# Conditioned residual layer on one core: tiles reordered on chip so that 25 pairs share a matrix, and the pair-matrix products done as seven half products

## The chip, the cores and the metric

The kernel runs on one core of a Trainium2 chip, in float32. The metric is the device time of one execution in microseconds (us), the median of several runs. The engines are called as in the profile: PE is TensorE's matmul, PEld its weight load, DVE is VectorE, ACT is ScalarE, POOL is GpSimd, and SP is the queue that issues most plain DMAs. L404 is line 404 of the kernel before.

## The reference, cut to what matters

The input `x` has 16 x 512 tokens of 512 features. Every token has a pathway id (500), a compartment id `c` (5, used also as time step) and a scale type `m` (3 in the tables; the mask that is passed in holds only 0 and 1).

```python
h = ln(x, pw_g[pathway], pw_b[pathway]);  h = ln(h, cp_g[c], cp_b[c])
t = ln(x, tm_g[c], tm_b[c]);              s = ln(x, ms_g[m], ms_b[m])
mm, n, r = [x + mlp_ln(state)[:, None, :] for state in (memory, noise, resource)]
cat = concat([w0*h, w1*t, w2*mm, w3*n, w4*r, w5*s], -1)       # w = softmax(aw)
out = x + ln(silu(cat @ int_W1 + int_b1) @ int_W2 + int_b2, int_g, int_be)
```

`t` and `s` are the same normalised `x` with another scale for each column. So for all tokens of one group (c, m) the two blocks of `int_W1` fold into one 512 x 512 matrix V = diag(w1 tm_g[c]) W1_t + diag(w5 ms_g[m]) W1_s. The three `x +` blocks fold into one matrix for `x`, and what hangs on batch and group becomes one added row for each token.

## The kernel before, in words

The kernel sorts the 8192 tokens on chip by group (15 groups, NG) and cuts the sorted list into 64 tiles of 128 tokens. The group of a tile is that of the token in its middle; tokens of another group at a border are put right by correction rows. A window is four tiles, and 16 windows are worked off one after another. In window w, tiles g = 0 and 2 are tiles 2w and 2w+1 of the sorted list, and g = 1 and 3 are tiles 32+2w and 33+2w (`by_place`, `PLACES`).

For a window, rows of `x` (`gx`), of the pathway table (`gh`), of the compartment table (`gc`) and the added rows (`ga`) are gathered by indirect DMAs from POOL. ACT and DVE make the sums and norms (`xs`, `f1`, `fs`, `f2`, `fn`, `nv`; the powers `xp`, `fp`, `lp` are POOL's). Each tile is turned in two steps: a 32 x 32 block transpose on DVE (`tx`, `tv`, `th`, `tz`, L197) and four DMAs of SP for each tile (`sX`, `sV`, `sH`, `sZ`, L205), which fill `catX`, `catV`, `catH`, `catZ`. All four block transposes of a window must be done before the first of its SP rows.

First layer, for each tile, three products of 128 x 512 by 512 x 512: with V (`lV`, `layer1`, L404, four matmuls of 512 columns, each of two records in the trace), and with the matrices of `x` and `h`. The last two are done from window 1 on as a Strassen-Winograd scheme: two tiles of a window form a pair p (tiles 2p and 2p+1), the two rows of a 2 x 2 block matrix whose columns are X and H. Seven products of half width (`m7.w.p.k`, `half_product`, L452, four matmuls of 256 columns each) stand for eight. DVE makes the token sums in place (`u1` to `u4`) and adds the parts that several results share (`r1`, `r2`, `r3`, `r5`, `half_out`). The V products and the parts that belong to one result gather in a PSUM bank for each tile (`p1`), the shared parts in a bank for each pair (`u`). Then come the sum with the gathered row (`ha`, L472), silu (`hs`, L475), turning (`tz`, `sZ`) and the second layer, seven products again (`q7.w.p.k`, L546, two matmuls of 256 columns each) with sums on POOL (`zs`, L532 to L538) and a bias put in first (`kb`, L520). The result is taken out of PSUM (`kf`, `sf`, `ku`, `sl`), normalised (`lq`, `lv`, `lp`, `lb`) and scattered to the output (`po`).

The V of a tile lies in `vs[g % 2]`. It is built only when the group changes from the tile of the same parity before: ACT writes W1_s scaled (`sp`, `s_part`, L257) and DVE adds W1_t scaled (`bd`, `build`, L265), both under a branch on a flag that is loaded into registers (`va`, `vd`).

The order of work on every engine is written out: `ORDER` for the start, `WINDOW` for each later window and `LAST` for the last one. A name such as `lV.c.1` is a piece for the current window (c; p is the window before, o the one before that, n the next, m the one after) and tile 1. Every engine takes its instructions strictly in that order. Before `ORDER`, a straight-line part counts the groups, gives every token its place (`pos`, L832), and makes the sorted list by comparing places with `i_q` (the tile numbers 0 to 63) and multiplying one-hot matrices on PE (`one_hots`, L883 to L896). From it come the gather indices `tok`.

Of the kernel before, what the change touches and what calls it, by code (L numbers as in the profile page):

```python
# [1548 lines left out]
```

## Time and profile before

| | |
|---|---|
| time, median of 3 runs | 923.6 us (922.99 to 923.74) |
| profiled execution, first to last instruction | 920.3 us |
| its own time: that span and about 3.3 us around it, taken from the median | about 923.6 us |
| PE busy | 884.8 us (96%) |
| PEld busy | 642.0 us (70%) |
| DVE busy | 733.6 us (80%) |
| ACT busy | 521.2 us (57%) |
| POOL busy | 666.9 us (72%) |
| DMA | 185.40 MB, mean 201 GB/s |
| builds of a V (L265 x44, four for each) | 11 |

A share of busy time is a mean over stages with different limits; the table by stage, asked for with stretches of about one window, says which engine has no room in which stage. The chain that ended last runs backwards from the last instruction to what released each step. Busy times there are counted once where records of one engine overlap, and the mean of one instruction is its whole record.

### The profile page before, as it was taken

The numbers are of one execution on the slowest core, as the hardware profiler recorded it, in microseconds if no ns is written. First come the engines' busy times: TensorE is split into PE (matmuls) and PEld (weight loads), VectorE is DVE, ScalarE is ACT, GpSimd is POOL, SyncE is SP. The second block draws the span as 40 slices with busy tenths as digits, with TensorE's granted clock in tenths as the row PEclk, the third lists the DMA queues.
The fourth block names the chain that finished last, engine by engine and source line by source line (L and its number), as shares of the span: only waits on it lengthen the run. The fifth ranks groups of instructions, "written<-read, shape, count | busy, mean of one in ns | idle before, by whom it ended". The sixth has DMA issues, their size and how long they took to land.

```text
span 920.3 us, 13563 instructions
## 1 busy us (share of the span) xinstructions
PE 884.8 (96%) x3617; PEld 642.0 (70%) x3617; DVE 733.6 (80%) x1360; ACT 521.2 (57%) x1263; POOL 666.9 (72%) x730
## 2 busy tenths in 40 slices
PE   6979899999999999999999999999999999999996
PEld 6634446868677777868686877777686867778682
DVE  8776767878789798978787887869697888879565
ACT  5568736464555738374646556473657566572413
POOL 9876678576768678686878686877767676876452
PEclk9999999999999999999999999999999999999999
DMA  8755677777767777777777777777667776776513
GB/s 272 249 185 179 220 226 197 207 210 204 235 178 232 202 218 195 215 208 202 227 202 227 187 235 191 226 193 216 186 197 210 203 220 191 221 200 190 154 37 113
DMA packets 88557, 185.40 MB, mean 201 GB/s; under 512 B 24324, under 2 KB 24388, under 8 KB 88476
## 3 DMA queue, kind: packets, MB, share of 16 engines
q0 software_dynamic: 31104, 104.88, 39.4%
q1 hardware_dynamic: 56668, 79.53, 29.6%
q8 instruction: 30, 0.49, 0.2%
q14 instruction: 51, 0.42, 0.2%
q10 hardware_dynamic: 704, 0.08, 0.1%
HBM read 100.48 MB, written 19.97 MB: 131 GB/s over the span
## 4 chain that ended last, share of the span: by engine, by line
PE 50%; POOL 5%; DVE 4%; issue 3%; DMA 3%; SPq 2%; ACT 1%; POOLq 0%; DVEq 0%; ACTq 0%
PE u L452 13%; PE p L404 13%; PE p L452 11%; PE pq_0b L546 4%; PE pq_1b L546 4%; PE pq_1a L546 3%; PE pq_0a L546 2%; SPq L205 2%; DMA catZ<-rZ 2%; POOL xbs L391 1%; POOL out L638 1%; DMA pw<-in_pw,i_pw 1%; DVE vs L265 1%; DVE yb L634 0%; DVE yb L633 0%
## 5 line engine op out<-in xcount | busy, mean ns | idle before, releaser
L404 PE MATMUL p<-vs,catV 128*128 128x512 f32 x512 | 228.3, 593 | 3.9 <-DVE vs L265 1.7
L404 PEld LDWEIGHTS p<-vs,catV 128*128 128x128 f32 x512 | 96.9, 190 | 108.5 <-issue 99.6
L452 PE MATMUL p<-wh__81,catH 128*128 128x256 f32 x480 | 111.0, 379 | 0.0
L452 PEld LDWEIGHTS p<-wh__81,catH 128*128 128x128 f32 x480 | 91.4, 190 | 12.2
L376 ACT ACTIVATE pw<-pw,rsh 128x512 f32<-128x512 f32 x64 | 45.6, 714 | 95.2 <-DVE pw L383 76.9
L638 POOL DMA_INDIRECT out<-yb,tok x64 | 75.4, 1178 | 31.2 <-issue 15.1
L475 ACT ACTIVATE add<-add 128x512 f32<-128x512 f32 x64 | 39.7, 625 | 94.4 <-DVE add L472 93.1
L350 ACT ACTIVATE junk<-pw 128x512 bf16<-128x512 f32 x60 | 37.5, 626 | 85.8 <-DVE pw L347 78.1
L171 POOL DMA_INDIRECT cp<-cp_rows,i_cp x64 | 73.4, 1147 | 15.5 <-issue 13.2
L391 POOL TENSOR_TENSOR xbs<-xbs,rows 128x512 f32<-128x512 f32 x64 | 82.4, 1289 | 1.4
L171 POOL DMA_INDIRECT pw<-in_pw,i_pw x64 | 63.0, 984 | 28.1 <-DVE rH L197 13.0
L625 POOL TENSOR_TENSOR rsy<-vey,mhalf 128x4 f32<-128x4 f32 (+1 forms) x16 | 23.6, 1473 | 82.3 <-DVE veh L368 69.5
L171 POOL DMA_INDIRECT xbs<-in_x,tok x64 | 65.1, 1017 | 19.9 <-issue 18.1
L171 POOL DMA_INDIRECT add<-rows,i_add x64 | 67.0, 1048 | 16.6 <-issue 16.5
L383 DVE SCALAR_TENSOR_TENSOR pw<-pw,sumsh,cp 128x512 f32<-128x512 f32 x60 | 45.5, 760 | 32.9 <-DMA cp<-cp_rows,i_cp 32.8
L317 ACT ACTIVATE xm<-xbs,nmx,rsx 128x512 f32<-128x512 f32 x64 | 48.8, 806 | 22.9 <-DVE nmx L311 17.2
L372 POOL TENSOR_TENSOR rsh<-veh,mhalf 128x1 f32<-128x1 f32 x64 | 48.6, 760 | 13.0 <-DVE veh L368 11.5
L347 DVE SCALAR_TENSOR_TENSOR pw<-pw,rsx 128x512 f32<-128x512 f32 x64 | 56.0, 876 | 2.3
L452 PE MATMUL p<-wt,catH 128*128 128x256 f32 x240 | 56.7, 379 | 0.0
L452 PE MATMUL u<-wt,catX 128*128 128x256 f32 x240 | 56.5, 379 | 0.0
L452 PEld LDWEIGHTS u<-wx__80,catX 128*128 128x128 f32 x240 | 45.7, 190 | 12.6 <-issue 3.8
L452 PE MATMUL u<-wt,ss 128*128 128x256 f32 x240 | 54.4, 379 | 0.0
(439 smaller groups left out, 2127.7 us busy)
## 6 DMA issues: line engine op xcount, KB each, us to landing
catX<-rX SPq DMA_DIRECT2D x240, 64.0 KB
catV<-rV SPq DMA_DIRECT2D x240, 64.0 KB
catZ<-rZ SPq DMA_DIRECT2D x240, 64.0 KB
catH<-rH SPq DMA_DIRECT2D x240, 64.0 KB
rows<-adde SPq DMA_DIRECT2D x8, 256.0 KB
yb<-in_int_W SPq DMA_DIRECT2D x1, 1024.0 KB
catH<-in_int_W SPq DMA_DIRECT2D x1, 1024.0 KB
w1x<-in_int_W SPq DMA_DIRECT2D x1, 1024.0 KB
```

The costliest lines, as they stand in the source:

```text
L171: nc.gpsimd.indirect_dma_start(dst, None, table, bass.IndirectOffsetOnAxis(ap=idx, axis=0), **kw)
L317: nc.scalar.activation(t, st["xb"][:, j, :], AF.Identity, bias=st["nm"][:, j : j + 1], scale=st["rs"][:, j : j + 1])
L347: nc.vector.scalar_tensor_tensor(h, h, st["rs"][:, j : j + 1], pw[:, D:], ALU.mult, ALU.add)
L372: nc.gpsimd.tensor_tensor(rs, st.pop(("ve", j)), mhalf[:, :1], ALU.pow)
L376: nc.scalar.mul(pw[:, :D], pw[:, :D], st.pop(("rs", j)))
L383: nc.vector.scalar_tensor_tensor(pw[:, :D], pw[:, :D], st["sh", j][:, 1], cp, ALU.add, ALU.mult)
L391: nc.gpsimd.tensor_add(st["xb"][:, j, :], st["xb"][:, j, :], rows[:, 2, :])
L404: nc.tensor.matmul(st["p1", g], st["c" + blk][:, g, c, :], m[:, c, :], start=(blk == first and c == order[0]), stop=(blk == last and c == ...
L452: nc.tensor.matmul(dst, m[:, c], at_["half1"][k][:, c], start=(k == 1 and c == 0), stop=(c == NC - 1), skip_group_check=True)
L475: nc.scalar.activation(st["add", g], st["add", g], AF.Silu)
L546: nc.tensor.matmul(st["pq", 2 * p + i][:, half], st["zp", p][k][:, c], at_["half"][k][:, c], start=False, stop=(c == 1), skip_group_check= ...
L638: nc.gpsimd.indirect_dma_start(out_rows[j], bass.IndirectOffsetOnAxis(ap=tok[:, j, w : w + 1], axis=0), yb[:, j, :], None)
```

## The change

The 64 tiles are put into another order. A group's tiles are taken two by two, all pairs come first, and tiles that are left over alone come last. This is worked out on chip: from the group borders follows how many tiles each group has, whether that is odd (`n_odd`), and with that the tile for each place (`i_q` is overwritten with it, and `by_place` now takes four places in a row for a window). At most 14 groups can have a tile alone, so 25 pairs (`PURE`) surely share one V. With the inputs of the reference the groups have 11, 11, 11, 11, 12, 1, 2, 2, 2 and 1 tiles; there are 29 such pairs, the other four are treated as single tiles.

For a pair that shares its V, the V product of both tiles is a product of a 2 x 2 block matrix (two tiles by two halves of the features) with V in four quarters, done by seven products of two matmuls with 256 columns (`v7.w.p.k`, `norm_product`). Its parts fall into the same places as those of `m7`, so both add up in the same PSUM halves. New sums of the turned tiles are made by DVE (`yv`, four of 128 x 256 for each pair, in the buffer of `rV`), and new sums of V's quarters by DVE when V is built (four more instructions; they take the place of `vs[1]`). The first shared part is no longer added by DVE (`r1` goes); ACT copies it from PSUM into both halves of the tile's bank before the other parts add up there (`cf`, `copy_first`). Places 50 to 63 use `lW` (`whole_product`), as `lV` before. Window 0 keeps whole products. So 23 pairs (windows 1 to 11, and the first of window 12) use `v7`.

`ORDER`, `WINDOW` and `LAST` are new; `LAST` writes out windows 12 to 15 by number, `ORDER` now reaches to the middle of window 1's work. The store of the sorted list to `in_order` becomes an indirect DMA on POOL behind the first gathers of `x`, because its rows are in the new order.

```diff
 WINDOW = """
+    m7.p.0.2 u4.p.0 fp.c.1 fn.c.1 u1.p.1 m7.p.1.2 m7.p.0.6 u4.p.1 m7.p.1.6 lp.o lb.o.3 kb.p.0 r2.p.0 kz.m.2 po.o.3 va.n
+    lb.o.0 gx.n.0 m7.p.1.5 sp.c.0 bd.c.0 m7.p.0.5 sh.p.0 r5.p.1 gc.c.3 lb.o.2 sV.c.3 gx.n.2 xs.n.0 gx.n.3 r3.p.1
+    m7.p.0.3 m7.p.1.4 th.c.1 ha.p.0 r2.p.1 u3.c.0 ha.p.3 hs.p.3 r3.p.0 gh.c.2 th.c.0 m7.p.0.4 ha.p.1 r5.p.0 hs.p.0
+    gh.c.3 hs.p.1 lb.o.1 tz.p.3 po.o.1 m7.c.0.1 v7.c.0.1 m7.p.1.3 tz.p.0 ha.p.2 po.o.2 cf.c.0 m7.c.0.7 v7.c.0.2 hs.p.2
+    sV.c.1 yv.c.0.3 gc.c.2 v7.c.0.7 kb.p.1 xs.n.3 tz.p.1 sh.p.1 sX.c.2 gx.n.1 tz.p.2 m7.c.1.1 ga.c.3 yv.c.0.1 cf.c.1
+    f1.c.2 v7.c.0.5 yv.c.0.2 yv.c.0.4 fs.c.2 f1.c.3 v7.c.0.3 fv.c.2 v7.c.0.6 sX.c.3 u3.c.1 ga.c.1 v7.c.0.4 sp.c.2 bd.c.2
+    v7.c.1.1 sZ.p.0 q7.p.0.1 q7.p.0.2 kz.p.1 fs.c.3 po.o.0 fv.c.3 fp.c.2 cf.c.2 m7.c.1.7 yv.c.1.3 f2.c.2 f2.c.3 sZ.p.1
+    xs.n.1 sh.c.3 fn.c.2 th.c.2 sZ.p.2 fp.c.3 fn.c.3 th.c.3 zs.p.0 tx.n.1 v7.c.1.7 q7.p.0.7 zs.p.1 q7.p.0.5 zs.p.2
...
+    PURE = (NT // P - (NG - 1)) // 2
...
+    def v_half(k):
+        if k in (4, 5, 6, 7):
+            return vs[1][:, {5: 0, 7: 1, 6: 2, 4: 3}[k]].rearrange("p (c n) -> p c n", c=2)
+        return vs[0][:, 2 * (k > 1) :, (k > 2) * (D // 2) :][:, :2, : D // 2]
...
+    def one_matrix(st, g):
+        return tile_of(st, g) - g % 2 < 2 * PURE
...
     def build(st, g):
-        w, v = st["w"], v_of(st, g)
+        if one_matrix(st, g) and g % 2:
+            return
+        w, v = st["w"], vs[g % 2]
...
                 nc.vector.scalar_tensor_tensor(v[:, c], wt[:, c], sct[:, c, g, w : w + 1], v[:, c], ALU.mult, ALU.add)
+            if one_matrix(st, g):
+                nc.vector.tensor_sub(v_half(5), b12, b11)
+                nc.vector.tensor_sub(v_half(7), b22, b12)
+                nc.vector.tensor_sub(v_half(6), b22, v_half(5))
+                nc.vector.tensor_sub(v_half(4), b21, v_half(6))
...
+    def norm_sum(st, p, k):
...
+            st["sv"] = catp.tile([P, 2, 4, 2, P], F32, tag="rotV", name=f"sv{st['w']}")
+        s1, s2, s3, s4 = [st["sv"][:, p, n] for n in range(4)]
+        a11, a12, a21, a22 = [st["cV"][:, 2 * p + r, 2 * n : 2 * n + 2] for r in range(2) for n in range(2)]
         if k == 1:
             nc.vector.tensor_add(s1, a21, a22)
         elif k == 2:
             nc.vector.tensor_sub(s2, s1, a11)
         elif k == 3:
+            nc.vector.tensor_sub(s3, a11, a21)
         else:
+            nc.vector.tensor_sub(s4, a12, s2)
...
+    def norm_product(st, p, k):
...
+        for c in range(2):
+            nc.tensor.matmul(dst, m[:, c], v_half(k)[:, c], start=(k == 5 and c == 0), stop=(c == 1),
+                             skip_group_check=True)
...
+    def copy_first(st, g):
...
+        nc.scalar.copy(st["p1", g].rearrange("p (k n) -> p k n", k=2),
+                       st["u", g // 2][:, :H].unsqueeze(1).to_broadcast([P, 2, H]))
...
-        if kind == "1":
-            nc.vector.tensor_add(a[:, :H], a[:, :H], u)
...
     def by_place(t):
-        return t.rearrange("p (b w a) -> p a b w", b=2, a=2)
+        return t.rearrange("p (w g) -> p g w", g=Q)
...
+    nc.vector.tensor_scalar(t_ends[:, 1:NG], row_beg, t_mid, None, ALU.is_gt)
+    nc.vector.tensor_sub(t_in, t_ends[:, 1:], t_ends[:, :NG])
     nc.vector.tensor_tensor(tmp, run, pc.unsqueeze(2).to_broadcast([P, NG, NQ]), ALU.add)
...
+    nc.tensor.matmul(pto[:NG, :1], t_in[:NQ], by_turns[:NQ], start=True, stop=True)
+    nc.scalar.activation(n_odd, pto[:NG, :1], AF.Square)
...
+    nc.vector.tensor_scalar(single, i_back[:NG], n_left, n_less, ALU.is_equal, ALU.mult)
...
+    nc.scalar.copy(i_q, pto[:, NQ : 2 * NQ])
...
+    for t, base in ((i_pos, 0), (i_mid, P // 2 - 1), (i_end, P - 1), (i_next, P)):
+        nc.gpsimd.tensor_scalar(t[:NB].rearrange("p (g w) -> p g w", g=Q), by_place(i_q[:NB]), float(P), float(base),
+                                ALU.mult, ALU.add)
...
-    nc.sync.dma_start(in_order.rearrange("(k r) o -> k (r o)", r=P), at_c)
...
     gather_x(w0)
+    nc.gpsimd.indirect_dma_start(in_order.rearrange("(k r) o -> k (r o)", r=P),
+                                 bass.IndirectOffsetOnAxis(ap=i_tile, axis=0), at_c, None)
...
-    for w in range(NW - 1):
+    for w in range(2, 12):
         run(WINDOW, w)
-    run(LAST, NW - 1)
+    run(LAST)
```

More of the change, by code (lines that the diff above doesn't have):

```diff
@@ L241, in changes, with tile_of @@
             skip_runtime_bounds_check_because="a comparison's result")
+    def tile_of(st, g):
+        return Q * st["w"] + g
+    def one_matrix(st, g):
+        return tile_of(st, g) - g % 2 < 2 * PURE
     def if_new(st, g, engine, part):
-        if st["w"] == 0 and g < 2:
+        if tile_of(st, g) in (0, 2 * PURE + 1):
             part()
@@ L260, in build @@
     def build(st, g):
-        w, v = st["w"], v_of(st, g)
+        if one_matrix(st, g) and g % 2:
+            return
+        w, v = st["w"], vs[g % 2]
+        H = D // 2
+        b11, b12, b21, b22 = [v[:, 2 * r : 2 * r + 2, k * H : (k + 1) * H] for r in range(2) for k in range(2)]
         def part():
@@ L404, in layer1 @@
             nc.tensor.matmul(st["p1", g], st["c" + blk][:, g, c, :], m[:, c, :],
-                             start=(blk == first and c == order[0]), stop=(blk == last and c == order[-1]),
-                             skip_group_check=st["w"] > 0)
+                             start=(blk == first and c == order[0]), stop=(blk == last and c == order[-1]))
     def awake(kind, at, n):
@@ L436, in token_sum, with home_of @@
         elif k == 3:
-            nc.vector.tensor_sub(a21, a11, a21)
+            nc.vector.tensor_sub(s3, a11, a21)
         else:
-            nc.vector.tensor_sub(a12, a12, s2)
+            nc.vector.tensor_sub(s4, a12, s2)
+    def home_of(st, p, k):
+        H = D // 2
+        key, half = {1: ("u", 0), 7: ("u", 0), 5: ("u", 0), 6: ("u", 1), 2: ("a", 0), 3: ("a", 1), 4: ("b", 0)}[k]
+        if key == "u":
+            if ("u", p) not in st:
+                st["u", p] = psum(f"u{st['w']}_{p}")
+            t = st["u", p]
+        else:
+            t = st["p1", 2 * p + (key == "b")]
+        return t[:, half * H : (half + 1) * H]
@@ new lines, in whole_product @@
+    def whole_product(st, g):
+        if one_matrix(st, g):
+            return
+        for c in range(NC):
+            nc.tensor.matmul(st["p1", g], st["cV"][:, g, c, :], vs[g % 2][:, c, :], start=False, stop=(c == NC - 1),
+                             skip_group_check=True)
+    def copy_first(st, g):
+        if ("p1", g) not in st:
+            st["p1", g] = psum(f"p1_{st['w']}_{g}")
+        H = D // 2
+        nc.scalar.copy(st["p1", g].rearrange("p (k n) -> p k n", k=2),
+                       st["u", g // 2][:, :H].unsqueeze(1).to_broadcast([P, 2, H]))
@@ L748 @@
     iota(i_rest[NH:], [[0, NQ]], base=NB1 - NH, step=1)
-    up = prep.tile([P, NG + 1], F32, name="up")
-    nc.gpsimd.memset(up[:, :1], 0.0)
     tokf = prep.tile([P, NE], F32, name="tokf")
@@ L783 @@
     nc.vector.memset(ones, 1.0)
+    odd_i = prep.tile([P, 1], I32, name="odd_i")
+    nc.vector.tensor_copy(odd_i, i_row)
+    nc.vector.tensor_scalar(odd_i, odd_i, 1, None, ALU.bitwise_and)
+    by_turns = prep.tile([P, 1], F32, name="by_turns")
+    nc.vector.tensor_copy(by_turns, odd_i)
+    nc.vector.tensor_scalar(by_turns, by_turns, -2.0, 1.0, ALU.mult, ALU.add)
     for v in range(2):
```

266 lines of the change are left out of this document (178 added, 88 removed).

## The prediction

> **What bounds the kernel now.** I read the page's busy shares first, then a table of stages one window long, then the chain that ended last inside a steady window.
>
> ```profile
> span 920.3 us, 13563 instructions
> PE 884.8 (96%) x3617; PEld 642.0 (70%) x3617; DVE 733.6 (80%) x1360; ACT 521.2 (57%) x1263; POOL 666.9 (72%) x730
> ...
> 313.20:363.20 50.00, 50.00 (x202) 38.08 (x201) 43.87 (x78) 30.69 (x75) 38.91 (x39) 1.00 0.75 216
> 363.20:413.36 50.16, 50.16 (x201) 37.98 (x201) 43.89 (x78) 30.71 (x75) 37.91 (x39) 1.00 0.72 208
> 463.35:513.35 50.00, 50.00 (x202) 38.07 (x201) 41.12 (x74) 28.46 (x71) 38.20 (x39) 1.00 0.75 213
> 563.50:613.50 50.00, 50.00 (x201) 38.10 (x201) 40.10 (x75) 28.30 (x71) 37.84 (x39) 1.00 0.73 209
> 613.50:667.00 53.50, 50.51 (x201) 37.91 (x201) 42.71 (x78) 31.16 (x76) 38.23 (x39) 1.00 0.71 202
> 667.00:719.00 52.00, 51.30 (x203) 38.29 (x203) 46.18 (x84) 34.10 (x81) 39.26 (x40) 1.00 0.72 203
> 719.00:769.46 50.46, 49.48 (x199) 37.47 (x198) 41.80 (x76) 29.55 (x73) 37.29 (x38) 1.00 0.71 205
> 769.46:820.36 50.90, 50.30 (x202) 37.89 (x201) 42.92 (x78) 30.70 (x75) 38.29 (x39) 1.00 0.72 208
> ```
>
> Columns after the stretch: its length, then busy time of PE, PEld, DVE, ACT, POOL, granted clock, DMA share, GB/s. A steady window lasts 50.0 us and PE is busy in all of it at full clock; DVE, next, has 40 to 41 us of work. The four stretches from 613.50 to 820.36 have 206.86 us and 201.59 us of PE: 5.3 us of stalls. The chain in a steady window is PE alone:
>
> ```profile
> 482.32 1.73 PE u L452 x8
> ...
> 489.23 6.87 PE p L404 x16
> ...
> 502.99 1.73 PE pq_0a L546 x8
> 504.71 1.73 PE pq_0b L546 x8
> 506.44 0.86 PE pq_0a L546 x4
> 507.30 1.73 PE pq_1a L546 x8
> ```
>
> Start, length, what: one `m7` product (L452) takes 1.73 us, two whole V products (L404) 6.87. One seventh-type product of two 256-column matmuls (L546, four records) takes 0.864 us.
>
> **The change, part by part.**
>
> *The products.* A pair costs 7 x 0.864 = 6.05 us instead of 6.87: 0.82 us less. 23 pairs: **-18.9 us** of PE, in the engine that sets the end. A steady window falls from 50.0 to 48.36 us of PE; windows 13 to 15 keep 50.0.
>
> *DVE.* These rows price its new work, and ACT's:
>
> ```profile
> L461 DVE TENSOR_TENSOR add<-add,u 128x256 f32<-128x256 f32 x30 | 12.1, 403 | 19.8 <-DMA add<-rows,i_add 17.8 <-PE p L404 1.9
> L574 DVE TENSOR_TENSOR yb<-yb 128x256 f32<-128x256 f32 x30 | 15.9, 530 | 2.7 <-ACT yb L569 2.7
> L574 DVE TENSOR_TENSOR yb<-yb x30: 381/410/982, 157.7 to 896.6; 128x256 f32<-128x256 f32 x30
> L433 DVE TENSOR_TENSOR ss<-catX,catH 128x512 f32<-128x512 f32 x30 | 19.4, 687 | 4.7 <-DMA catV<-rV 2.3 <-DMA catH<-rH 2.3
> L265 DVE SCALAR_TENSOR_TENSOR vs<-wt,sct,vs 128x512 f32<-128x512 f32 x44 | 30.2, 748 | 1.5 <-ACT vs L257 1.5
> L257 ACT ACTIVATE vs<-ws,scs 128x512 f32<-128x512 f32 x44 | 28.1, 710 | 1.8 <-PE p L404 1.5 <-ACTq L248 0.2
> L520 ACT COPY pq_0a<-rows 128x512 f32<-128x512 f32 x15 | 8.7, 579 | 0.0
> ```
>
> The third row has the shortest, median and longest of one. A window gains eight `yv` (nearest row L574, as both inputs lie in SBUF; median 0.41 us) and loses two `r1` (L461, 0.40): +2.5 us, so 42.6 of 48.36 us. That leaves 5.8 us idle, where the stretch at 667.00 also had 5.8 (46.18 of 52.00) and PE lost 0.7. I take 0.2 us a window, ten windows: **+2**; bounds 0 and 7.
>
> *ACT.* Four copies `cf` a window; a copy of 512 columns into PSUM is 0.58 us (L520): +2.3 on 28.5 of 48.4, hidden beside PE as work. As a wait: the product behind each copy (`m7.c.0.7`, `v7.c.0.5`) has one other product of 1.73 us between, longer than 0.58. I take 0; if ACT stands in a row of sums when the copy is due, 1 us a window at most. What queues behind a `cf` on ACT is the silu of the window before.
>
> *Builds.* L265 x44 is 11 builds; the counts of tiles make it 18 after: 5 among the shared pairs (four in the loop, at windows 2, 5, 7 and 10), 13 from place 51 on. A shared build also has four more DVE instructions of 512 columns (L433, 0.69). At windows 5 and 10 it comes ahead of some 20 us of `m7` products: 0. At windows 2 and 7 (`sp.c.2 bd.c.2` directly before `v7.c.1.1`) both matrices are in use until the first pair is nearly done: 0.71 of ACT and 4 x 0.75 of DVE is 3.7 us, less 1.7 of products still running: 2 us each, **+4**; bounds 0 and 8.
>
> *Late windows.* From the middle of window 12 every tile has its own V. Windows 13 and 14 have four builds each: DVE 40.1 - 0.8 + 4 x 2.99 = 51.3 us against 50.0 of PE. `LAST` pushes the four `lb` of window 13 behind. Windows 12 to 14 come to 3 x 39.3 + 11 builds x 2.99 + 4 `yv` x 0.41 - 5.8 (the `lb`) = 146.6 us of DVE in 149 of PE, 98%; the nearest row, 46.18 of 52.00, is 89%. If DVE's 5.8 us idle are needed in each, the three lose 14; if none, 0. I take **+6**. The stalls of the old order between 613.50 and 820.36 go with it: **-5** (0 if they return).
>
> *Start.* The comparison with `i_q` must now wait for the tile order.
>
> ```profile
> 8.27 1.16 DVE L829 TENSOR_TENSOR vs<-vs,pc 128x960 f32<-128x960 f32 x1 [0.49 <-PE pc L811]
> 9.15 0.32 PE L815 MATMUL pbg<-room,up 128*14 128x1 f32 x6 [0.92 <-POOL tokf L752]
> 10.10 0.15 ACT L826 COPY begs<-pbg 128x14 f32<-128x14 f32 x1
> 10.65 1.79 DVE L832 TENSOR_REDUCE pos<-vs 128x64 f32<-128x960 f32 x1
> 13.35 1.23 DVE L883 TENSOR_TENSOR vs<-catZ 128x1024 f32<-128x1024 f32 x1
> 15.30 0.52 POOL L926 TENSOR_SCALAR rows<-room,begs 14x64 f32<-14x64 f32 x1
> 15.80 1.94 POOL L927 TENSOR_SCALAR rows<-room,begs 14x64 f32<-14x64 f32 x1
> 35.11 0.18 POOL L987 TENSOR_TENSOR of_seg<-t,c 14x1 f32<-14x1 f32 x1
> 36.56 1.24 POOL L171 DMA_INDIRECT xbs<-in_x,tok  x1 [1.27 <-PE ptp L1014]
> ```
>
> `t_ends` now stands before L829 on DVE and needs the copy that ended at 10.25; the memset of `up` that L815 waited for on POOL (0.92 us) is moved ahead, which brings the copy to about 9.4. So L829 starts 1.4 us later, three small DVE instructions behind the PE/ACT steps add 0.6, and L883 comes at 15.4 instead of 13.35. The small products and copies of the tile order on PE and ACT (L815 and L826 are their size) lie beside L829 to L832 except for those 0.6. POOL gets four instructions of the kind of L926 and L927 (0.52 to 1.94 us each) that need `i_q`: its chain to L987 ends 3 us later or more, and the first gather (36.56) with it. I take **+2.5** (bounds 0, if window 0's cover holds, and 7). The store to `in_order` goes from SP to POOL behind four gathers, 1 us of issue; the gathers behind it wait that long, inside the bounds.
>
> *Tail.*
>
> ```profile
> L633 DVE SCALAR_TENSOR_TENSOR yb<-yb,rsy,rows 128x512 f32<-128x512 f32 x56 | 43.2, 771 | 0.0
> L634 DVE TENSOR_TENSOR yb<-yb,xbs 128x512 f32<-128x512 f32 x56 | 38.7, 692 | 1.9
> 897.46 13.97 PE L487 MATMUL p<-w,catV 128*128 128x512 f32 x32
> ```
>
> After the last PE product the old chain has 8.9 us (911.4 to 920.3). The new one sends four `lb.14` (L633 and L634, 1.46 us each on DVE) just before the sums of the last window: **+1**; bounds -1 and +3.
>
> Sum: -18.9 + 2 + 4 + 6 - 5 + 2.5 + 1 = -8.4. Span 920.3 - 8.4 = 911.9; with the 3.3 us that lie between the profiled span and the median of 923.6: **915 us**.
>
> **The rivals.**
>
> *The cover holds everywhere* (faster still): the steady windows lose nothing, builds hide, only the start is paid: 923.6 - 18.9 + 2 = 906.7; without that 905. For it: the stretches from 313.20 and 363.20, with 43.9 us of DVE, cost PE nothing. Against it: 98% in the late windows.
>
> *The turned hidden tiles come late* (slower). In the old order the first `q7` has 13.7 us between the last `m7` and itself; in the new one 9.5 (`m7.c.0.7` to `v7.c.1.1`: two of 1.73, seven of 0.864).
>
> ```profile
> 439.07 7.03 PE L404 MATMUL p<-vs,catV 128*128 128x512 f32 x16
> 442.67 1.48 DVE L197 STREAM_TRANSPOSE rZ<-add 128x512 f32<-128x512 f32 x2
> 444.21 10.06 SPq L205 DMA_DIRECT2D catZ<-rZ  x16
> 453.32 0.73 POOL L532 TENSOR_TENSOR yb<-catZ 128x256 f32<-128x256 f32 x1 [1.15 <-DMA catZ<-rZ]
> ```
>
> The last `m7` ends at 439.1, SP starts its 16 row DMAs at 444.2 (0.63 us each), POOL waits until 453.3 for tiles 0 and 1. Eight issues end at 449.2, so landing takes 4.1 us; tile 0 is there at about 450.8, 11.7 us after the `m7`. The new order has fewer steps before SP (two adds, a silu, two transposes: 3.1 instead of 5.1), 9.7 against 9.5. Each us above 9.5 is lost in each of 11 windows; from 11.1 a window is no shorter than 50.0. At the old 11.7 it is 50.56, and 11 x 2.2 us come on my sum less its 2 for steady windows: about 937.
>
> *DVE becomes the bound.* With 42.6 us of work it decides from 7.4 us of idle that it cannot use; the stretch at 463.35 idles 8.9, though most of that is waiting for a PE that is itself full. At 7.9 a window is 50.5: about 935.
>
> *The new sums meet POOL* (no change). L574 has a mean of 0.530 us over a median of 0.410, because single ones reach 982 ns, about two lengths: one that waits for another engine's whole instruction. At the mean, eight `yv` make DVE's window 43.6 us; with the 5.8 us of idle of the stretch at 667.00 it lasts 49.4, ten windows are 10.4 us longer than 48.36, and 915 - 2 + 10.4 is 923. For it: POOL has 38 us of work in each window. Against it: half of L574 ran at 0.41 or less beside that same POOL.
>
> The page "SBUF — State Buffer" of the Trainium skill, section "Who interferes with whom", states a rule that gives this: a DVE instruction with two SBUF inputs and a POOL instruction that reads SBUF shut each other out, and the later waits for the whole of the earlier. The 982 ns agrees with it; by the rule every `yv` that meets a POOL sum would go as in this rival, and the sum would be 923 in place of 915.
>
> That the halves don't come cheaper is excluded by L546's row; that pairs don't share, by the counts of tiles.
>
> **How the numbers follow.** My forecast has 0.62, with its own range 907 to 921.5; full cover 0.16; sums that meet POOL 0.08; hidden tiles 0.07; DVE 0.07. A difference under 0.2% (1.8 us) cannot be told from none here. Faster 0.78, same 0.08, slower 0.14. The range 905 to 924 leaves the two slow cases out.
>
> **What would show it.** A steady window of 48.4 to 49 us with PE full, V in 14 products of 0.86; DVE at 42 to 44 us; waits of PE for `build` at windows 2 and 7; stretches of windows 12 to 14 with PE idle and DVE near full; the first L883 at about 15.4. Wrong it is if PE idles before `q7` in every window, or if the late windows lose more than 15 us.

## The result and the profile after

The changed kernel takes **1017.26 us** (median of four runs, 1015.46 to 1021.03) against 923.3 (921.51 to 923.74): a ratio of 1.1037, 95% interval 1.1002 to 1.1073. I had forecast 915 us, 905 to 924. It is 94 us slower where I said 8 us faster.

The page of the kernel after, its first lines, the slices of DVE and of the granted clock, and the chain by engine:

```profile
span 1013.5 us, 14659 instructions
...
PE 904.0 (89%) x3908; PEld 702.9 (69%) x3909; DVE 882.7 (87%) x1476; ACT 573.6 (57%) x1357; POOL 675.5 (67%) x735
...
DVE  8576568979999999999999999999987979799886
...
PEclk9989999989999999999999999899999899899998
...
DVE 29%; PE 21%; issue 11%; SPq 8%; ACT 7%; DMA 4%; another core or an unknown queue 2%; POOL 1%; ACTq 0%; DVEq 0%; POOLq 0%
```

PE was the bound at 96% and now idles 109.5 of 1013.5 us. DVE is at nine tenths or more in every slice of the middle, and it leads the chain. It has 116 more instructions than the 1360 of before (9%), but 149 us more busy time than 733.6 (20%): its instructions have become longer, not only more.

The table by stage after, one row from the first product `m7.w.0.1` of a window to that of the next, here windows 3, 4, 5, 6, 10, 12 and 14; columns as before:

```profile
263.67:315.33 51.66, 49.81 (x225) 41.94 (x224) 47.48 (x80) 30.30 (x74) 35.98 (x37) 1.00 0.74 205
315.33:368.23 52.90, 49.71 (x225) 42.08 (x224) 50.51 (x79) 33.04 (x78) 36.40 (x36) 1.00 0.70 200
368.23:425.62 57.39, 51.05 (x225) 43.34 (x224) 54.86 (x89) 30.55 (x74) 40.19 (x40) 0.97 0.65 183
425.62:478.92 53.30, 49.63 (x225) 42.01 (x224) 50.45 (x80) 30.23 (x73) 38.41 (x38) 1.00 0.68 200
...
640.62:697.26 56.64, 51.04 (x226) 43.93 (x224) 53.74 (x89) 30.39 (x74) 40.00 (x40) 0.94 0.66 185
751.96:816.67 64.71, 56.25 (x213) 43.09 (x212) 57.24 (x89) 37.37 (x84) 43.82 (x41) 0.89 0.54 157
...
873.27:933.63 60.36, 50.51 (x185) 36.14 (x184) 51.93 (x79) 37.65 (x80) 34.45 (x35) 0.92 0.59 171
```

A plain window lasts 51.7 to 53.3 us with DVE 47.5 to 50.5 us busy, where I had 48.4 and 42.6. A window with a build lasts some 57 us. The late windows lose most, and with a low granted clock.

Three single instructions show why DVE is longer; each row has shortest, median and longest of one in ns (the second and third are the new sums `yv`), then the instruction of POOL they meet:

```profile
L424 DVE SCALAR_TENSOR_TENSOR pw<-pw,rsx x64: 750/752/2334, 64.7 to 942.6; 128x512 f32<-128x512 f32 x64
L527 DVE TENSOR_TENSOR sv<-catV x23: 379/883/2194, 154.7 to 759.0; 128x256 f32<-128x256 f32 x23
L531 DVE TENSOR_TENSOR sv<-catV x23: 402/416/3105, 155.5 to 758.7; 128x256 f32<-128x256 f32 x23
L468 POOL TENSOR_TENSOR xbs<-xbs,rows x64: 1251/1275/1723, 133.4 to 986.1; 128x512 f32<-128x512 f32 x64
```

And one such meeting in the timeline (start, length):

```profile
292.50 1.24 POOL L662 TENSOR_TENSOR zs<-catZ 128x256 f32<-128x256 f32 x1
293.20 2.33 DVE L424 SCALAR_TENSOR_TENSOR pw<-pw,rsx 128x512 f32<-128x512 f32 x1
293.71 1.25 POOL L468 TENSOR_TENSOR xbs<-xbs,rows 128x512 f32<-128x512 f32 x1
```

L424 starts while a sum of POOL (L662) runs, and ends 0.57 us after the next one (L468, `sh`, which adds a row to the gathered `x`): 0.75 us of work took 2.33, as if it had stood still through both.

PE's own waits after (in all, times, longest):

```profile
PE u L553 <- ACT p L580: 20.3, 8, 5.4
PE pq_1b L672 <- DVE yb L691: 17.5, 12, 3.1
...
PE u L565 <- DVEq L315: 6.3, 1, 6.3
PE p L565 <- DVE sv L533: 6.3, 6, 1.1
PE p L572 <- ACT p L580: 6.2, 1, 6.2
```

L580 is the copy `cf` that I had put at nothing, L691 a sum of the second layer on DVE, L315 the branch of a build.

### The profile page after: what moved, and what is told of

Read it like the earlier page. It is cut to its first block, busy times and chain, and to the rows that moved or that the text cites. A ratio compares the mean times of both kernels' runs of the same rounds, so it can differ in the third digit from the quotient of the medians.

```text
span 1013.5 us, 14659 instructions
## 1 busy us (share of the span) xinstructions
PE 904.0 (89%) x3908; PEld 702.9 (69%) x3909; DVE 882.7 (87%) x1476; ACT 573.6 (57%) x1357; POOL 675.5 (67%) x735
## 4 chain that ended last, share of the span: by engine, by line
DVE 29%; PE 21%; issue 11%; SPq 8%; ACT 7%; DMA 4%; another core or an unknown queue 2%; POOL 1%; ACTq 0%; DVEq 0%; POOLq 0%
SPq L263 8%; PE u L553 6%; PE p L572 4%; PE p L553 3%; DMA catX<-rX 3%; DVE rV L255 3%; PE u L565 2%; PE pq_0b L672 2%; DVE pw L460 2%; DVE pw L423 2%; DVE sv L531 2%; DVE rX L255 2%; DVE vs L337 2%; ACT junk L738 2%
## 5 line engine op out<-in xcount | busy, mean ns | idle before, releaser
L764 POOL DMA_INDIRECT out<-yb,tok x64 | 69.7, 1089 | 67.0 <-issue 28.8
L553 PE MATMUL p<-wh__81,catH 128*128 128x256 f32 x480 | 111.4, 379 | 0.0
L553 PEld LDWEIGHTS p<-wh__81,catH 128*128 128x128 f32 x480 | 91.1, 190 | 13.0 <-issue 0.7
L229 POOL DMA_INDIRECT xbs<-in_x,tok x64 | 63.4, 990 | 48.5 <-DVE yb L760 27.6
L427 ACT ACTIVATE junk<-xbs 128x512 bf16<-128x512 f32 x64 | 40.1, 626 | 97.2 <-DMA xbs<-in_x,tok 73.4
L449 POOL TENSOR_TENSOR rsh<-veh,mhalf 128x1 f32<-128x1 f32 x64 | 48.2, 756 | 53.9 <-DVE veh L445 53.3
L468 POOL TENSOR_TENSOR xbs<-xbs,rows 128x512 f32<-128x512 f32 x64 | 83.5, 1309 | 0.5
L553 PE MATMUL u<-wt,catX 128*128 128x256 f32 x240 | 64.4, 417 | 21.3 <-ACT p L580 20.3
L601 ACT ACTIVATE add<-add 128x512 f32<-128x512 f32 x64 | 38.7, 626 | 76.6 <-DVE add L598 42.6
L565 PE MATMUL u<-vs,sv 128*128 128x256 f32 x276 | 70.1, 384 | 7.7 <-DVE sv L531 3.7
L553 PEld LDWEIGHTS u<-wt,catX 128*128 128x128 f32 x240 | 48.6, 207 | 34.3 <-ACT p L580 25.1
L424 DVE SCALAR_TENSOR_TENSOR pw<-pw,rsx 128x512 f32<-128x512 f32 x64 | 64.5, 1007 | 3.2 <-POOL rsx L377 0.9
L598 DVE TENSOR_TENSOR add<-p,add 128x512 f32<-128x512 f32 x64 | 42.2, 665 | 26.7 <-remote 19.8
L394 ACT ACTIVATE xm<-xbs,nmx,rsx 128x512 f32<-128x512 f32 x64 | 49.4, 805 | 28.1 <-DVE nmx L388 18.9
L337 DVE SCALAR_TENSOR_TENSOR vs<-wt,sct,vs 128x512 f32<-128x512 f32 x72 | 64.7, 957 | 0.4 <-ACT vs L325 0.4
L565 PEld LDWEIGHTS u<-vs,sv 128*128 128x128 f32 x276 | 50.9, 190 | 20.0 <-DVE sv L531 5.1
L453 ACT ACTIVATE pw<-pw,rsh 128x512 f32<-128x512 f32 x64 | 44.5, 714 | 34.5 <-POOL rsh L449 15.4
L759 DVE SCALAR_TENSOR_TENSOR yb<-yb,rsy,rows 128x512 f32<-128x512 f32 x60 | 57.5, 959 | 1.6 <-POOL rsy L751 1.6
```

Source lines behind the costliest of these rows:

```text
L229: nc.gpsimd.indirect_dma_start(dst, None, table, bass.IndirectOffsetOnAxis(ap=idx, axis=0), **kw)
L337: nc.vector.scalar_tensor_tensor(v[:, c], wt[:, c], sct[:, c, g, w : w + 1], v[:, c], ALU.mult, ALU.add)
L394: nc.scalar.activation(t, st["xb"][:, j, :], AF.Identity, bias=st["nm"][:, j : j + 1], scale=st["rs"][:, j : j + 1])
L424: nc.vector.scalar_tensor_tensor(h, h, st["rs"][:, j : j + 1], pw[:, D:], ALU.mult, ALU.add)
L427: nc.scalar.activation(junk, x, AF.Identity, accum_out=sums[:, 0, k : k + 1])
L468: nc.gpsimd.tensor_add(st["xb"][:, j, :], st["xb"][:, j, :], rows[:, 2, :])
```

## The experiments

The reasons weighed: DVE's work is stretched by POOL's shifts (`sh`); the builds stand in DVE's row ahead of work that PE needs; the new sums `yv` are too much for DVE; the copies `cf` come late by their place.

One thing has to be read with every comparison. The runs were made on four chips: no_shift, shift_dve, no_sums and cf_early on chip 13; no_builds, light, shift_placed and before_sums on chip 10; placed_no_builds, no_four, seed_first and builds_early on chip 2; only_sums, only_builds, only_shift and busy_pe on chip 1. In all eight runs of chips 13 and 2, and in after, whose chip is not on record, DVE's sums `ha` and ACT's copies `cf` wait 14 to 24 us in all for an event for which the trace names no releaser ("remote"). None of the eight runs of chips 10 and 1 has such a wait. The rows of after and of no_sums (there the lines are two lower):

```profile
DVE add L598 <- remote: 19.8, 4, 6.4
```
```profile
ACT p L578 <- remote: 9.0, 3, 3.5
DVE add L596 <- remote: 5.3, 1, 5.3
```

They are called nameless waits here. They lie in window 2 and in windows 12 to 14, in seed_first also in windows 3, 8 and 9. So a time with them and a time without them cannot be set against each other as they stand. Where two runs differ in this, the text also gives their windows 3 to 11, from the first product of window 3 to that of window 12, which but for seed_first hold no such wait: 488.3 us in after. The kernel before is not slower on chips 13 and 2 (921.1 and 921.4 us) than on 10 and 1 (922.3 and 922.4).

### Parts taken away or moved, one at a time

**no_shift**

```diff
-    nc.gpsimd.tensor_add(st["xb"][:, j, :], st["xb"][:, j, :], rows[:, 2, :])
+    pass
```

> The changed kernel without the 64 shifts (the POOL sums of x and a constant row): the shift of x is left out of the result. Collision theory (DVE sets the steady windows because its sums of two SBUF inputs are held up by POOL's sums, 86 of about 120 us of lengthening beside the shifts alone): DVE's busy time falls by 70 to 90 us to about 800, its steady window to 42 to 44 us, the steady window of the kernel from 52-57 us to 49-51, and the time to 935-960. Rival, the work theory (DVE's own added sums and builds, and the order, make it late; the lengthening is only what fills waiting): DVE's lengthening moves to the other POOL sums and the time stays above 1000. Rival, the copy theory (TensorE waits for the copies cf that stand behind silus on ACT): above 1005.

Measured 976.05 us, ratio to before 1.057 (1.0509 to 1.0631): 41 us less than after. Its page:

```profile
PE 896.0 (92%) x3909; PEld 703.3 (72%) x3909; DVE 796.6 (81%) x1476; ACT 570.6 (58%) x1357; POOL 588.9 (60%) x671
```

DVE has the same 1476 instructions and 86.1 us less busy time. No work of DVE was taken away: that is what POOL's 64 shifts cost it.

**shift_dve**

```diff
-    nc.gpsimd.tensor_add(st["xb"][:, j, :], st["xb"][:, j, :], rows[:, 2, :])
+    nc.vector.tensor_add(st["xb"][:, j, :], st["xb"][:, j, :], rows[:, 2, :])
```

> The changed kernel with the 64 shifts on DVE instead of POOL. DVE gets 64 more instructions of 512 columns, 0.69 us each, 44 us. Collision theory: the engine that sets the time gets more work and the kernel still becomes faster, since 86 us of lengthening go: DVE about 840 us, the time 965 to 990. Work theory: 44 us more on the engine that sets the time: 1040 to 1060.

1003.11 us, 1.0875 (1.0821 to 1.093). Even with 64 more instructions on it (1540), DVE is busy for 833.2 us, 49.5 less than after: doing the shift costs DVE less than meeting it. The time gained is 14 us, less than I expected of the collisions.

**no_sums**

```diff
     def norm_sum(st, p, k):
+        return
...
-        m = left[k] if k in left else st["sv"][:, p, {5: 0, 6: 1, 7: 2, 3: 3}[k]]
+        m = left[k] if k in left else v[:, 2 * p + 1, :2]
```

> The changed kernel without the DVE sums yv: the half products that should read them read an unsummed quarter instead, so V's products are computed from other numbers; the count of matmuls is the same. Collision theory: the 92 sums took 75 us, twice their undisturbed 38, so DVE falls by some 75 us and the time to 945-970. Work theory: only the undisturbed 38 us are won, 3.3 us in each of ten windows: 980 to 990. Copy theory: no change beyond the few us that TensorE waits for yv directly, 1000 to 1015.

1006.67 us, 1.0924 (1.0871 to 1.0978). Only 10.6 us come back, so the new sums are not the main cause (windows 3 to 11: 476.8 for 488.3).

**cf_early**

```diff
-gh.c.3 hs.p.1 lb.o.1 tz.p.3 po.o.1 m7.c.0.1 v7.c.0.1 m7.p.1.3 tz.p.0 ha.p.2 po.o.2 cf.c.0 m7.c.0.7 ...
+gh.c.3 lb.o.1 tz.p.3 po.o.1 m7.c.0.1 v7.c.0.1 m7.p.1.3 cf.c.0 hs.p.1 tz.p.0 ha.p.2 po.o.2 m7.c.0.7 ...
```

> The changed kernel with one silu moved behind the first copy of each window on ACT (the copy no longer waits for the second tile's sums on DVE). Copy theory: the 20 to 26 us in which TensorE waits for the copies go: 990 to 1000. Collision theory: TensorE's wait only moves to the next thing that DVE brings late: 1007 to 1020.

1019.36 us, 1.104 (1.0986 to 1.1095): no different from after. PE's wait for the copies (L553) falls from 20.3 to 15.9 us, and nothing is gained: the place of `cf` against one silu is not the cause.

**no_builds**

```diff
-                else:
+                elif st["w"] < 1:
```

> The changed kernel without the builds of V's matrices from window 1 on (ACT's and DVE's part of each): V is computed from stale matrices. Build theory (each build, up to 8 more DVE instructions between the sums that TensorE waits for, costs a stall and a slow stretch of TensorE behind it): windows 2, 5, 7 and 10 come down from 57-61 us to the 52-53 of their neighbours, windows 12 to 14 from 57-65 to 51-54, the start by 6: 960 to 975. Collision theory: builds matter only by DVE's busy time, 3 to 6 us in each place, and the late windows stay above 55: 985 to 995.

966.72 us, 1.0503 (1.0459 to 1.0547): 50.5 us less, but after has its nameless waits in this difference and no_builds has none. In windows 3 to 11 it gains 14.7 us (473.6 for 488.3). Against busy_pe (below), which does all the work of after and has no nameless wait either, it is 28.6 us less. Builds cost far more than my +4 and +6.

**light**: no_shift, no_sums and no_builds together.

> The changed kernel without POOL's shifts, without the sums yv and without the builds from window 1 on, all three left out together: V and the residual are computed from other numbers. What remains is the new order with its half products and copies. If shifts, sums and builds are all that is wrong: steady windows of 48.4 to 49 us and a time of 910 to 925. Order theory (V's products now hang on the seed product and its copy, so that TensorE has lost the 13.7 us of products that covered the hidden layer's sums, and the start and the late windows wait): steady windows of 50 or more, 935 to 955.

915.65 us, 0.9947 (0.9922 to 0.9972). Without the three things the new order is not slower than the kernel before. After is 101.6 us above it, nameless waits included; in windows 3 to 11 it is 48.1 us (488.3 for 440.2).

**shift_placed**: the same shifts at other places of the row.

```diff
-sh.p.0 ... sh.p.1 ... sh.c.3 ... sh.c.2
+gc.c.3 sh.p.0 ... gx.n.3 sh.p.1 ... gh.c.3 sh.p.2 ... fp.c.3 sh.p.3
```

> The changed kernel with the four shifts of a window at other places of POOL's queue, all behind the sums that read x and ahead of the last sums: one each behind the last gathers gc and gh of the window, one behind the last gather of x, one behind the last power of front, where in the trace DVE runs transposes and sums that read PSUM. Same work everywhere. Collision theory: most of the gain of leaving the shifts out, 41 us, comes back: 978 to 995, DVE busy 810 to 840 us. Rival (it is POOL's work and not its meeting with DVE): 1010 to 1020.

972.82 us, 1.0551 (1.0519 to 1.0583). With every instruction of after it is 44 us faster, but it has none of after's nameless waits (19.8 us). In windows 3 to 11 it gains 19.6 us (468.7 for 488.3), nearly as much as leaving the shifts out (466.9 in no_shift); DVE falls from 882.7 to 835.0. It is the fastest kernel here that does the whole work on the new order, and still slower than before. Its windows 4 to 6:

```profile
309.80:359.60 49.80, 49.40 (x226) 42.13 (x225) 43.69 (x79) 32.46 (x78) 37.69 (x37) 1.00 0.74 211
359.60:416.20 56.60, 50.88 (x225) 43.57 (x224) 52.66 (x89) 30.80 (x76) 39.49 (x40) 0.94 0.67 187
416.20:466.80 50.60, 49.42 (x226) 42.23 (x225) 44.22 (x80) 29.74 (x74) 39.36 (x39) 1.00 0.72 210
```

The plain windows come down to 50, the window with a build stays at 56.6.

**before_sums**: the kernel before, with the eight sums `yv` in windows 2 to 11, spread over the row (nothing reads them).

```diff
+    yv.c.0.1 (behind sp.c.3) yv.c.0.2 (fs.c.3) yv.c.0.3 (fv.c.3) yv.c.0.4 (zs.p.0)
+    yv.c.1.1 (kf.p.0) yv.c.1.2 (xs.n.2) yv.c.1.3 (ku.p.0) yv.c.1.4 (zs.p.3)
```

> The kernel before with eight more DVE sums a window in windows 2 to 11, the same sums of two SBUF inputs as the change's, written to a tile that nothing reads. Collision theory: DVE's 9 idle us of a window take them even where single ones are lengthened: 921 to 927. Work theory (eight more sums at their places fill DVE): 935 or more.

922.77 us, 1.0019 (0.9997 to 1.0041), though DVE is busy 766.6 us in place of 733.6. In the old order eight more sums a window are free.

### Builds, looked at closer

**placed_no_builds**: shift_placed and no_builds together.

> The changed kernel with the shifts at their other places and without the builds from window 1 on (V from stale matrices). If shifts, builds and sums cost each their own share (44, 50 and 11 us when taken singly): 1017 - 44 - 50 = 923, the kernel before within some us, steady windows of 49 to 50. If the two causes feed one another (a build costs only because the collisions have used up DVE's slack, or the other way round): more than 935, as then the shares taken singly count the same loss twice.

969.12 us, 1.0544 (1.0479 to 1.0609): no faster than shift_placed or no_builds, but it has nameless waits (21.6 us at `ha` and `cf`) and they have none. In windows 3 to 11 it takes 451.0 us, against 468.7 in shift_placed and 473.6 in no_builds: there each of the two edits gains beside the other. Its plain windows last 49.4 to 50.4 us, but windows 12 to 14 take 58.2, 59.6 and 56.1, with no build in them, and window 2 takes 56.5; all four hold nameless waits.

**no_four**: the four added sums of V's quarters left out of each shared build.

```diff
-            if one_matrix(st, g):
+            if one_matrix(st, g) and st["w"] < 1:
```

> The changed kernel without the four DVE sums that a shared build adds (20 instructions of 0.68 us in five builds, one of them in window 0 kept): V's half products read stale sums of the matrix. If they are what makes the builds dear: the four windows with a shared build and window 12 lose 3 to 4 us each, 15 to 20 in all: 997 to 1002. If a build's price is its place, between the sums that the seed's copy waits for, whatever its length: 5 to 10 us, 1007 to 1012.

1007.58 us, 1.0931 (1.0872 to 1.099). Windows 5, 7 and 10 take 54.9, 54.0 and 55.0 in place of 57.4, 56.6 and 56.6: 1.6 to 2.6 us for 4 x 0.69 = 2.8 us of DVE. In these windows most of what a build takes on DVE counts. Against that, window 14, with a nameless wait of 7.6 us, got 3.1 us longer, and the whole time fell by 9.7 us only.

**seed_first**: shift_placed, and `lb.o.1`, `lb.o.2` with their stores moved behind the copy and the silus. **builds_early**: that, and the builds of windows 1 and 12 earlier.

```diff
-m7.p.0.5 ... lb.o.2 ... gx.n.2 ... hs.p.0 ... hs.p.1 lb.o.1 tz.p.3 po.o.1 m7.c.0.1 v7.c.0.1 m7.p.1.3 tz.p.0 ha.p.2 po.o.2 cf.c.0 m7.c.0.7 v7.c.0.2 hs.p.2
+tz.p.3 m7.c.0.1 v7.c.0.1 m7.p.1.3 cf.c.0 hs.p.0 hs.p.1 tz.p.0 ha.p.2 m7.c.0.7 v7.c.0.2 hs.p.2 lb.o.1 po.o.1 lb.o.2 po.o.2 gx.n.2
...
-kz.0.1 xs.2.1 sV.1.0 wz
+kz.0.1 xs.2.1 sV.1.0 sp.1.0 bd.1.0 wz
...
-m7.11.1.5 po.10.1
+m7.11.1.5 bd.12.0 po.10.1
```

> The changed kernel with the shifts at their other places, and in each window the first copy ahead of two silus on ACT and two of the last sums (lb, 1.43 us each on DVE) behind the hidden tiles' sums. Build theory (DVE's queue is late at the copy by the length of the build, 6 us, and PE idles 5.6 us): with 2.9 us less ahead of it and the copy freed of two silus, windows 2, 5 and 10 fall from 53-57 to 51-53 and the time by 6 to 12 us against the kernel with the shifts moved: 961 to 967. Rival (TensorE then waits for the next thing that DVE owes): 970 to 976.

> The kernel of the run before this one, and the builds of windows 1 and 12 moved ahead of the hidden tiles' sums, where before TensorE waited for them at the first V product (6.3 and 4.3 us). Build theory: some 4 to 8 us less than the run before: 955 to 962. Rival (the build then delays the sums and TensorE waits as long for the copy): no change.

1007.58 us, 1.0929 (1.0869 to 1.0989), and 1003.21 us, 1.0892 (1.0833 to 1.095): both some 30 us slower than shift_placed, which they start from, but both have nameless waits (21.2 and 14.7 us) and shift_placed has none. In windows 3 to 11 seed_first takes 487.4 us in place of 468.7, with 7.7 us of such waits among them. builds_early is 4.4 us faster than seed_first, the low end of what I expected. PE's waits of seed_first:

```profile
PE u L565 <- DVE sv L531: 18.0, 10, 3.3
...
PE u L553 <- ACT p L580: 5.6, 2, 3.5
```

The wait for `cf` fell from 11.3 us in shift_placed to 5.6, and a new one of 18.0 took its place: the moved `lb` now stood on DVE ahead of `yv.3`, which the next half product needs.

### Each suspect alone

**only_sums**, **only_builds**, **only_shift**: light, with one of the three put back.

> The changed kernel without POOL's shifts and without the builds from window 1 on; the sums yv stay. Against the kernel without all three (915.7 us) only the 92 sums come back. If DVE's slack hides them, as the prediction had it (2 us): 915 to 920. If each of the three causes keeps the share it had when it alone was taken out (11 us): 924 to 930.

> The changed kernel without the shifts and without the sums; the builds stay. Against 915.7 us only the builds come back. Build theory (a build costs a long stall at its place with or without collisions): 945 to 965, windows 2, 5, 7, 10 and 12 to 14 longer by 4 to 10 us each. Interplay theory (a build costs only when collisions have eaten DVE's slack): 920 to 930.

> The changed kernel without the sums and without the builds from window 1 on; the shifts stay on POOL at their places. Against 915.7 us only the collisions of the shifts with DVE's other sums come back. If the collisions cost by themselves: 945 to 960, steady windows of 51 to 52. If DVE's slack takes them as long as there are no sums and no builds: 916 to 925, steady windows of 48.5 to 49.

With these all eight combinations are measured (us; ratio to before with its interval):

| kept of the three | us | ratio | nameless waits | windows 3 to 11, us |
|---|---|---|---|---|
| none (light) | 915.65 | 0.9947 (0.9922 to 0.9972) | no | 440.2 |
| sums | 915.49 | 0.993 (0.9912 to 0.9947) | no | 440.0 |
| builds | 938.42 | 1.0181 (1.016 to 1.0202) | no | 450.7 |
| shifts | 955.09 | 1.0365 (1.0328 to 1.0401) | no | 464.1 |
| sums, builds (no_shift) | 976.05 | 1.057 (1.0509 to 1.0631) | yes | 466.9 |
| sums, shifts (no_builds) | 966.72 | 1.0503 (1.0459 to 1.0547) | no | 473.6 |
| builds, shifts (no_sums) | 1006.67 | 1.0924 (1.0871 to 1.0978) | yes | 476.8 |
| all (after) | 1017.26 | 1.1037 (1.1002 to 1.1073) | yes | 488.3 |

Alone the sums cost nothing, the builds 22.8 (between the two ranges that I had expected) and the shifts 39.4: 62.0 of 101.6, all from runs without nameless waits. The other 39.6 us are not all interplay. Busy_pe (below) keeps all three without a nameless wait and takes 995.28, 79.6 above light: by this, as an estimate, since it has useless products besides, some 18 us exist only where the three come together and some 22 go with the nameless waits. Windows 3 to 11 give 48.1 us for all three, of which 34.0 are there alone and 14.0 only together.

*Shifts.* The same instruction and the same sums of light and of only_shift and only_sums (min, median, max in ns), light first:

```profile
L424 DVE SCALAR_TENSOR_TENSOR pw<-pw,rsx x64: 750/752/1105, 62.1 to 841.6; 128x512 f32<-128x512 f32 x64
```
```profile
L424 DVE SCALAR_TENSOR_TENSOR pw<-pw,rsx x64: 750/752/3381, 62.0 to 877.5; 128x512 f32<-128x512 f32 x64
```
```profile
L531 DVE TENSOR_TENSOR sv<-catV x23: 412/416/425, 152.1 to 688.9; 128x256 f32<-128x256 f32 x23
```

Without shifts the longest L424 is 1.1 us, with them 3.4; without shifts every L531 lies between 412 and 425 ns. One plain window of light, only_sums, only_shift and no_builds (sums and shifts), in this order:

```profile
439.40:487.90 48.50, 48.50 (x225) 42.48 (x224) 40.08 (x72) 30.34 (x75) 33.46 (x35) 1.00 0.75 216
```
```profile
440.70:489.20 48.50, 48.50 (x225) 42.46 (x224) 43.25 (x80) 30.46 (x75) 32.99 (x35) 1.00 0.73 216
```
```profile
455.90:507.10 51.20, 49.31 (x225) 42.14 (x224) 44.21 (x72) 30.44 (x75) 37.92 (x38) 1.00 0.71 205
```
```profile
460.50:513.20 52.70, 49.75 (x225) 42.06 (x224) 50.47 (x80) 30.45 (x74) 38.30 (x38) 1.00 0.69 198
```

DVE's busy time is 40.1; the eight sums add 3.2 (0.40 each), the shifts 4.1 with no instruction more, and both together 10.4, since the sums are met too. In only_sums PE is still busy in all of the window; in no_builds DVE's 50.5 us don't fit into 48.5 any more. But only_shift's 44.2 us would fit, and its window is 2.7 us longer all the same. A DVE that still has idle time costs PE something when a stretched instruction stands ahead of a sum that PE needs; in only_shift these are above all the sums of the second layer:

```profile
PE pq_1b L670 <- DVE yb L689: 18.0, 11, 2.2
```


*Builds.* What a build does to its window is plain in only_builds, window 5 (timeline, all engines; without `norm_sum` the lines from there on are two lower than in after: L578 is after's L580, L599 its L601, L551 its L553):

```profile
340.31 2.73 DVE L337 SCALAR_TENSOR_TENSOR vs<-wt,sct,vs 128x512 f32<-128x512 f32 x4
342.96 0.69 DVE L339 TENSOR_TENSOR vs<-vs 128x512 f32<-128x512 f32 x1
...
344.89 0.69 DVE L342 TENSOR_TENSOR vs<-vs,vs 128x512 f32<-128x512 f32 x1
...
350.99 0.63 ACT L599 ACTIVATE add<-add 128x512 f32<-128x512 f32 x1 [3.71 <-DVE add L596]
353.11 1.15 ACT L599 ACTIVATE add<-add 128x512 f32<-128x512 f32 x2 [1.49 <-DVE add L589]
354.16 0.58 ACT L578 COPY p<-u 128x512 f32<-128x512 f32 x1
...
349.94 1.89 PE L551 MATMUL p<-wh__81,catH 128*128 128x256 f32 x8
354.79 3.30 PE L551 MATMUL u<-wt,catX 128*128 128x256 f32 x8 [2.97 <-ACT p L578]
357.88 1.45 PE L563 MATMUL p<-vs,catV 128*128 128x256 f32 x4
```

DVE builds from 340.31 to 345.6. The sums of the window before (`r`, `ha`) stand behind in its row and come that much later; ACT waits 3.71 and 1.49 us for them with its silus (L599); the copy `cf` (L578) stands behind the silus in ACT's row; PE waits 2.97 us for the copy. Then its next product takes 3.30 us where the same one takes 1.89, and the one behind it 1.45 for 1.03. In light the copy of that window came in time:

```profile
344.96 0.57 ACT L578 COPY p<-u 128x512 f32<-128x512 f32 x1 [0.32 <-PE u L563]
```

and the product of 354.79 started at 346.49, right behind the one before. The window of only_builds:

```profile
347.40:400.80 53.40, 50.43 (x226) 43.48 (x225) 44.24 (x80) 29.41 (x73) 35.59 (x37) 0.97 0.70 199
```

It is 4.9 us longer than light's 48.5: 2.97 of idle PE and 1.93 more of busy PE (50.43 for 48.50), with a granted clock of 0.97.

**busy_pe**: after, with five useless products in windows 2, 5 and 10 where PE idles, so that the clock doesn't fall.

```diff
+        if (p, k) == (1, 3) and st["w"] + 1 in (2, 5, 10):
+            for n in range(5):
+                nc.tensor.matmul(nx["p1", 0], wt[:, n % NC, :P], wt[:, n % NC], start=True, stop=True, ...)
```

> The changed kernel with five useless products (0.86 us each, 4.3 us) on TensorE in windows 2, 5 and 10, at the place where it idles 4.5 to 5.4 us for the first copy; they write the bank that the copy then overwrites. Clock theory (TensorE runs at half speed for some us after an idle time of more than about 3 us, which costs 3.4 us each time): three stalls no longer cool it, granted clock 1.00 in these windows instead of 0.94 to 0.97, the time 6 to 11 us less, 1006 to 1011. Rival (the useless products only delay the copy): 1017 to 1025.

995.28 us, 1.0798 (1.0781 to 1.0814). Its windows 2, 5 and 12:

```profile
202.30:260.50 58.20, 54.92 (x235) 43.72 (x235) 52.22 (x87) 32.70 (x79) 36.01 (x36) 1.00 0.63 178
364.30:421.70 57.40, 53.88 (x235) 44.07 (x234) 54.86 (x89) 30.55 (x74) 40.24 (x40) 1.00 0.64 183
748.50:806.90 58.40, 52.30 (x213) 40.73 (x212) 55.87 (x87) 36.43 (x82) 42.56 (x40) 0.97 0.60 170
```

The time lies in neither of the two ranges that I had expected. The clock is full in the three windows that got products (2, 5 and 10), but windows 5 and 10 are not shorter than in after, window 5 with the same 54.86 us of DVE. There the lost clock had cost nothing by itself. Window 2 is shorter (60.73 before the edit), but after has a nameless wait of 5.5 us in it and busy_pe has none, so that the clock did this is not shown. Most of the 22 us came in windows 12 to 14 (58.5, 51.4 and 54.2 for 64.7, 56.6 and 60.4), where nothing was put in. There, too, nameless waits of after are gone, as in every run of chip 1, so the 22 us cannot be called the work of this edit. One of these waits in after:

```profile
879.93 0.69 DVE L598 TENSOR_TENSOR add<-p,add 128x512 f32<-128x512 f32 x1 [6.44 <-remote]
...
875.64 1.24 PE L553 MATMUL u<-wx__80,catX 128*128 128x256 f32 x5
...
883.07 3.46 PE L572 MATMUL p<-vs,catV 128*128 128x512 f32 x4 [6.18 <-ACT p L580]
```

The sum L598 waits 6.44 us for an event without a releaser; by the program it needs PE's products alone, and PE's last listed one ends at 876.9. Then ACT's copy and PE wait for it. The semaphore that L598 waits on is PE's. In the trace's semaphore events it stands still from 870.0 to 879.9, while four products that post to it are listed as ended between 871.7 and 876.9. In the nine runs with nameless waits 113 to 168 of PE's posts come over 0.5 us after the listed end of their matmul, in no other run more than 10. After has four of these waits at L598 (19.8 us), no_shift three (17.6), placed_no_builds four (17.6). **Open** stays why PE posts late there, or is listed too early (the 2% of "another core or an unknown queue" in the chain of after), why all eight runs of two chips have it and none of the other two, and whether light, which was timed on chip 10 alone, would have it elsewhere.

## Why the prediction was wrong, by its own steps

*Products, -18.9: right.* The steady window, with nothing in the way, is 48.50 us of full PE in light (forecast 48.36). Over the whole span light has PE busy for 874.5 us, 10.3 less than before; some 6 us of the difference to 18.9 are clock (0.987 granted over 911.5 us in place of 0.994 over 920.3: 11.8 against 5.5 us).

*Light's 915.65 is not my 915 come true.* My sum without its terms for DVE, builds, late windows is 923.6 - 18.9 - 5 + 2.5 + 1 = 903. Light is 12 above: half of it that clock, the rest mostly in window 1, where PE waits for the DMAs of `catV`, in light too:

```profile
PE u L563 <- DMA catV<-rV: 4.6, 1, 4.6
```

*DVE, +2: the step that failed.* The eight sums are what I priced them at, 0.40 us, and alone they cost nothing (only_sums, before_sums). What failed is the 5.8 us of slack: I took DVE's other work as it was before, but it was the old places of POOL's shifts that left it so. In the new order the shifts meet L424, L759, the builds and the sums; plain windows have 47.5 to 50.5 us of DVE and not 42.6. In windows 3 to 11 the shifts alone cost 23.9 us, and with the sums 33.4, where I had 2 for ten windows.

*ACT's copies, 0, at most 1 us a window: right without builds, wrong with them.* Light waits 1.7 us in all before L551's and L563's products; after waits up to 5.4 at once. I wrote that the silu queues behind `cf`. What matters stands the other way: `cf` queues behind the silus, and these behind whatever DVE has in front of their sums.

*Builds, +4, none of it at windows 5 and 10: failed.* In only_builds the windows 2, 5, 7 and 10 are 3.2, 4.7, 0.9 and 4.6 us longer than in light: 13.5. Windows 2 and 7 together come to my +4, one above and one below its 2; windows 5 and 10 cost 9.3 where I had 0. I had looked at who reads V, and there my 20 us of cover for windows 5 and 10 is real. I had not asked what else stands behind a build in DVE's row.

*Late windows, +6 less 5: mis-sized in company.* Windows 12 to 14 take 147.9 us in light and 156.7 with builds alone, near my 149 + 6; with everything 181.7 in after, where nameless waits are 14.4 of it, and 164.1 in busy_pe, which has none. That is 15 above 149, just past my bound of 14. What the nameless waits add was in no term of mine.

*Start, +2.5: right in size as far as I worked it out.* The first L1047 (L883 before) starts at 15.37, forecast 15.4; the first product of the first layer is 4.7 us later (73.74 for 69.08), within 0 to 7. Window 1's wait for `catV` was not foreseen.

*Tail, +1:* from the first product of window 15 to the end 79.87 us, before 81.13: -1.3, just past the bound of -1.

*The rivals.* "The new sums meet POOL" had the right mechanism, and I gave it 0.08 and priced it on the eight new sums only, at 0.53 us each. The mean of L527 is 1.2 us in after, and the larger part falls on instructions that were there all along. The page that I quoted there, "SBUF — State Buffer" of the Trainium skill, section "Who interferes with whom", speaks of any DVE instruction with two SBUF inputs, and the 86.1 us of no_shift agree with it; I applied it to the new ones. "DVE becomes the bound" came true for another reason than mine: not idle that it cannot use, but longer instructions. "The turned hidden tiles come late" did not occur. That PE's clock would fall after a long stall was in no term: for the same products PE is busy for 904.0 us in after and 874.5 in light.

## What to carry to other kernels

When an order is rewritten, every two-input instruction of DVE gets new neighbours on POOL: count the meetings of all of them, not those of the added ones; moving four POOL additions a window was worth 19.6 us in nine windows here. Slack that an old order shows is not slack of the new one, and terms that each fit into the same slack must be summed before they are called hidden. For an instruction put into an engine's row ask not only who reads its result, but what stands behind it in the row and who waits for that. And before two times are set against each other, look in both traces for what differs besides the edit: here some 20 us of waits went with the chip that a run was made on.
